# Second layer of a two-layer Mamba block: preparation restructured as a pipeline, accumulating stores spread over the steps, four-state weights two steps ahead

## The chip, the cores and the metric

The kernel runs on one core of a Trainium2 chip (trn2). The metric is the device time of one launch in microseconds (us). The engines are PE (TensorE, with PEld for its weight loads), DVE (VectorE), ACT (ScalarE), POOL (GpSimd) and SP (SyncE, which only issues transfers here). Each works through its own queue in order.

## The reference

Four images of 64 x 64 positions and 192 channels pass through two layers. Each layer normalises groups of channels, projects to 384 inner channels, runs selective scans over four orders of the positions, sums the four results, normalises, gates and projects back. The change lies in the second layer, whose scan is this, run on four orders of the same sequence (rows, rows reversed, columns, columns reversed):

```
x_dbl = u @ W_x
dt, B_mat, C_mat = split(x_dbl)                 # 12, 16 and 16 columns
dt = softplus(dt @ W_dt + b_dt)
A = -exp(A_log)                                 # A[d, n], 16 states n
log_decay = cumsum(dt * A, axis=1)
decay = exp(log_decay)
dB_u = dt * B_mat * u
h = decay * cumsum(dB_u / (decay + 1e-12), axis=1)
y = einsum('bldn,bln->bld', h, C_mat) + u * D   # summed over the four orders
```

The term 1e-12 makes `h` vanish once the decay is small against it. The kernel therefore computes only the first positions of each order: 256 for state 0, 128 for states 1 to 3, 64 for states 4 to 7 and 32 for states 8 to 15. A running maximum, `alive`, records whether that was enough; if not, a slower path at the end recomputes the layer.

## The kernel before

The first layer takes most of the launch, and the change leaves it alone. The second layer, class `SecondLayer`, runs in four stages, each over all four images: `project`, `prepare`, `scans`, `finish`. A tile of [128, 3, 512] holds 384 channels (3 groups of 128 partitions) for 512 positions, which are four stretches of 128, one for each order. An image has two such chunks: M (the first 128 positions of each order) and E (the next 128).

**`project`** ends with convolutions whose result `u` goes out through tiles `du` (L1116, stored by L1119) into `y`, and whose first positions go to the DRAM tensors `uc`.

**`prepare`** turns each of the eight chunks (M and E of four images) into what the scans need. The instructions of one chunk, with their lines, are:

- SP loads `uc` (L1219); PE computes `xp` (L1222, three matmuls over 128 rows), ACT copies it with a bias to `xd` (L1224).
- `delta`, the softplus: PE computes `dp` for each of three channel groups (L1148, over 13 rows); ACT takes `Abs` (L1155), then `Exp` (L1156); POOL makes `wl`, `dt` and a correction (L1159 to L1161); ACT takes `Ln` (L1162); POOL adds (L1163). PE computes the three `dp` a second time, and DVE makes `dt = max(dp, 0) + e` (L1165). The `dp` tiles come from three PSUM buffers, so a `dp` can only be written once the third before it has been read.
- `sums`: DVE's running sum `cum` of `dt` (helper line L977). The E chunk continues from the M chunk's ends. `test` (L1191 to L1194) updates `alive`. DVE forms `e = dt * uc` (L1229).
- `keep`: PE transposes part of `xd` to `bp` (L1201) and the whole of `e` to `tp` (L1209, twelve transposes); ACT copies that to `dtuT` (L1210); SP stores `rows`, `bT`, `dtuT`, `dt` and `cum` in DRAM (L1198 to L1213).

In this stage a scheduler places the instructions on the engines' queues. It starts from the order of the program, which finishes one chunk before it begins the next.

**`scans`** has its order written out by hand. `flat` lists nine steps for each image: states 0, 1, 2, 3 on M one at a time; states 4-5 and 6-7 on S (half stretches); state 0 on E; states 8-11 and 12-15 on Q (quarter stretches). Four states together are called a four-state step here. In step `g` the queues get, in this order:

- `c_rows(g + 2)` (SP loads `bct`, L1320) and `b_product(g + 2)` (ACT, `xT`, L1314);
- `weight(g + 1)` and `decay(g + 1)`, the factors `sg` and `a` of the next step. With one or two states ACT makes them (L1284). With four states POOL first multiplies (L1273, six instructions), and ACT applies the function (L1279);
- for each channel group `d`: `scan(g, d)` on DVE (L1332 and two or four scans of L977), `turn_x(g + 1, d)` on PE (`x`, L1325, in three PSUM buffers), and, two steps behind (`LAG`), PE's sum of the products: `add_y` (`yp`, L1366), or for the E step `ext_y` (`yq`, L1383, copied by ACT to `yte`, L1384);
- `c_product(g)` on POOL (L1348), which multiplies the scan's `h` by `bct`.

Two results go out for each image: `yte` after its E step and `ytm` (copied from `yp` by `end_y`) when all steps are summed, two steps into the next image. Both call `store`, which puts six DMAs with addition on POOL's queue (L1400 for rows, L1403 for columns). They add to overlapping places of the same `y`, so some of them wait until earlier ones have landed.

```python
for k, lo in enumerate((near, near, L - far, L - far)):
    if k % 2 == 0:
        nc.gpsimd.dma_start(ys[b][lo : lo + SEG, :], y[:, k, :], accum_op=ALU.add)
        continue
    for s in range(2):
        nc.gpsimd.dma_start(v[lo // HW + s], y[s * HW : (s + 1) * HW, k, :], accum_op=ALU.add)
```

**`finish`** loads `y` again, normalises it (POOL, L891), gates it and projects it back (L916). Its first load of `y` (L870) was issued right after the last store of the scans had landed.

Of the kernel before, what the change touches and what calls it, by code (L numbers as in the profile page):

```python
# [979 lines left out]
class SecondLayer(FirstLayer):  # L980
# [149 lines left out]
    def prepare(self, ucs, batches):  # L1130
        nc, tc = self.tc.nc, self.tc
        with ExitStack() as ctx:
# [12 lines left out]
            def dt_rows(xd, d):  # L1145
                dp = ps_d.tile([128, LC], F32, name="dp")
                w = self.w_dt[:, 0, d * 128 : (d + 1) * 128]
                nc.tensor.matmul(dp, w, xd[0 : DR + 1, :], start=True, stop=True)  # L1148
                return dp

            def delta(xd):

                e = p3.tile([128, ND, LC], F32, name="e")
                for d in range(ND):
                    nc.scalar.activation(e[:, d, :], dt_rows(xd, d), AF.Abs)  # L1155
                nc.scalar.activation(e, e, AF.Exp, scale=-1.0)  # L1156
                wl = p2.tile([128, ND, LC], F32, name="wl")
                dt = p3.tile([128, ND, LC], F32, name="dt")
                nc.gpsimd.tensor_scalar(wl, e, 1.0, 1.0, ALU.add, ALU.mult)  # L1159
                nc.gpsimd.tensor_scalar(dt, wl, -1.0, 1.0, ALU.add, ALU.mult)  # L1160
                nc.gpsimd.tensor_tensor(e, e, dt, ALU.subtract)  # L1161
                nc.scalar.activation(wl, wl, AF.Ln)  # L1162
                nc.gpsimd.tensor_tensor(e, e, wl, ALU.add)  # L1163
                for d in range(ND):
                    nc.vector.scalar_tensor_tensor(dt[:, d, :], dt_rows(xd, d), 0.0, e[:, d, :], ALU.max, ALU.add)  # L1165
                return dt, e

            def sums(dt, before):

                cum = p3.tile([128, ND, LC], F32, name="cum")  # L1170
                for d in range(ND):
                    for k in range(KD) if before is not None else range(2):
                        w = SEG if before is not None else LC // 2
                        part = slice(k * w, (k + 1) * w)
                        if before is None:
                            scan_add(nc, cum[:, d, part], self.keep[:, part], dt[:, d, part], 0.0, k == 1)
                        else:
                            one = self.one.to_broadcast([128, SEG])
                            scan_add(nc, cum[:, d, part], one, dt[:, d, part], ends(before, d, k), k >= 2)
                return cum  # L1180
# [31 lines left out]
                nc.sync.dma_start(chunk.dram["dt"], dt)  # L1212
                nc.sync.dma_start(chunk.dram["cum"], cum)  # L1213

            for uc_dram, (main, ext, _, _) in zip(ucs, batches):
                before = None
                for r, chunk in enumerate((main, ext)):
                    uc = p2.tile([128, ND, LC], F32, name="uc")
                    nc.sync.dma_start(uc, uc_dram[:, r])  # L1219
                    xp = ps_x.tile([NX, LC], F32, name="xp")  # L1220
                    for d in range(ND):
                        nc.tensor.matmul(xp, self.w_xp[:, d, 0, :], uc[:, d, :], start=(d == 0), stop=(d == ND - 1))  # L1222
                    xd = p2.tile([NX, LC], F32, name="xd")
                    nc.scalar.activation(xd, xp, AF.Identity, bias=self.xbias)  # L1224
                    dt, e = delta(xd)
                    cum = sums(dt, before)
                    before = cum
                    test(cum, r)
                    nc.vector.tensor_mul(e, dt, uc)  # L1229
                    if r == 0:  # L1230
                        for at in (0, SEG, 3 * SEG - 1, 4 * SEG - 1):
                            nc.vector.memset(dt[:, :, at : at + 1], 1e30)
                    keep(chunk, xd, dt, cum, e)


    def scans(self, batches, ys):
        nc, tc = self.tc.nc, self.tc
        with ExitStack() as ctx:
            pool = lambda name, bufs, **k: ctx.enter_context(tc.tile_pool(name=name, bufs=bufs, **k))
            p1, p2, p3, p5 = (pool(f"s{b}", b) for b in (1, 2, 3, 5))  # L1240
            ps_y = pool("psy", 1, space=bass.MemoryType.PSUM)
            ps_x = pool("psx", 3, space=bass.MemoryType.PSUM)
            ps_m = pool("psm", 2, space=bass.MemoryType.PSUM)
# [47 lines left out]

            def weight(g):

                sg[g] = p3.tile([128, ND, LC], F32, name="sg")
                by_state(g, flat[g][0].cum, sg[g], AF.Tanh, 0.5, self.ln_q)

            def decay(g):
                as_[g] = p3.tile([128, ND, LC], F32, name="a")
                by_state(g, flat[g][0].dt, as_[g], AF.Exp)

            def blocks(g):
# [20 lines left out]
            def turn_x(g, d):  # L1322
                xs[g, d] = ps_x.tile([128, LC], F32, name="x")
                for b, (cols, _, _) in enumerate(blocks(g)):
                    nc.tensor.transpose(cols(xs[g, d]), xTs[g][:, b, d * 128 : (d + 1) * 128], ident)  # L1325
# [50 lines left out]
            def ext_y(g, b):  # L1376
                it = flat[g][0]
                if b == 0:
                    it.y = p1.tile([128, NJ, DI], F32, name="yte")
                yq = ps_m.tile([128, LC], F32, name="yq")  # L1380
                for q in range(b * NJ, (b + 1) * NJ):
                    k, d = divmod(q, ND)
                    nc.tensor.transpose(yq[:, q % NJ * 128 : (q % NJ + 1) * 128], hs[g][:, d, k * SEG : (k + 1) * SEG], ident)  # L1383
                nc.scalar.copy(it.y.rearrange("p j e -> p (j e)")[:, b * LC : (b + 1) * LC], yq)  # L1384
                if b == ND - 1:
                    store(it.y, flat[g][2], SEG)

            def end_y(b):
                y = p1.tile([128, NJ, DI], F32, name="ytm")
                for i in range(ND):  # L1390
                    to = y.rearrange("p j e -> p (j e)")[:, i * LC : (i + 1) * LC]
                    (nc.scalar.copy if i == 1 else nc.vector.tensor_copy)(to, yp[i])
                store(y, b, 0)

            def store(y, b, near):
                far = near + SEG
                v = ys[b].rearrange("(h w) e -> w h e", w=HW)
                for k, lo in enumerate((near, near, L - far, L - far)):
                    if k % 2 == 0:
                        nc.gpsimd.dma_start(ys[b][lo : lo + SEG, :], y[:, k, :], accum_op=ALU.add)  # L1400
                        continue
                    for s in range(2):
                        nc.gpsimd.dma_start(v[lo // HW + s], y[s * HW : (s + 1) * HW, k, :], accum_op=ALU.add)  # L1403

            with tc.manual_schedule(engines={nc.tensor.engine, nc.scalar.engine, nc.vector.engine, nc.gpsimd.engine}):
                tc.keep_in_program_order(nc.scalar.preload_act_table_set("exp_and_others"))
                for it in batches[0]:
                    load(it)
                c_rows(0)
                c_rows(1)  # L1410
                b_product(0)
                b_product(1)
                weight(0)
                decay(0)
                for d in range(ND):
                    turn_x(0, d)
                start_y()
                for g in range(N + LAG + 1):
                    b, n = divmod(g, PER)

                    for at, i in ((4, 0), (6, 2), (7, 1), (8, 3)):
                        if n == at and b + 1 < len(batches):
                            load(batches[b + 1][i])
                    if g + 2 < N:
                        c_rows(g + 2)
                        b_product(g + 2)
                    if g + 1 < N:
                        weight(g + 1)
                        decay(g + 1)
                    if n == 3 and 0 < b < len(batches):  # L1430
                        start_y()
                    ready = [g - LAG] if LAG <= g < N + LAG else []
                    if n == LAG and b > 0:
                        ready = []
                    elif n == 3 and b > 0:
                        ready = [g - 3, g - 2]
                    for d in range(ND):
                        if g < N:
                            scan(g, d)
                        if g + 1 < N:  # L1440
                            turn_x(g + 1, d)
                        for q in ready:
                            (ext_y if flat[q][0].name[0] == "E" else add_y)(q, d)
                    if g < N:
                        c_product(g)
                    if n == LAG and b > 0:
                        end_y(b - 1)


@with_exitstack  # L1450
# [126 lines left out]
```

## Time and profile before

| | us |
|---|---|
| median of three runs | 11391.58 (11390.1 to 11404.04) |
| the profiled execution: its own time | 11400.69 |
| its span from first to last instruction | 11398.9 |
| stage `prepare`: first L1148 to last L1210 | 10534 to 10728 |
| stage `scans`: first L1332 to last store | 10746 to 11093 |
| stage `finish` | 11095 to 11399 |

| engine | busy us, share of the span |
|---|---|
| PE | 9629.2 (84%) |
| DVE | 9660.8 (85%) |
| ACT | 9638.7 (85%) |
| POOL | 9049.1 (79%) |

The shares are averages over a launch in which the first layer has the greatest weight. The change touches some 550 us of it, so that stretch is read by itself: which engine waits for which, stage by stage. Times on the trace count from the first instruction. The mean granted clock of PE is 0.926 over the whole span, and lower in the second layer.

### The profile page before, as it was taken

To read this page: it belongs to the slowest core of one execution; us is meant where nothing else is said; L and a number is where in the kernel's file an instruction comes from. 1 tells how busy PE (TensorE), PEld (TensorE's weight loads), DVE (VectorE), ACT (ScalarE), POOL (GpSimd) and SP (SyncE) were. 2 spreads that over 40 slices of the span, in tenths; PEclk is the share of its full clock that TensorE was granted. 3 is DMA by queue.
4 is the path that set the end of the run, shared out by engine and by line. 5 is a ranking of instruction groups with operands and counts; after the bars stand their busy time and mean duration, and the time that the engine had idled before them with its cause. 6 is when DMAs were issued, how large, how long until landed. Compare 5 with 4: busy or idle time off the path is not lost. (4 is left out here: it accounts for less than half of the span.)

```text
span 11398.9 us, 171795 instructions
## 1 busy us (share of the span) xinstructions
PE 9629.2 (84%) x61449; PEld 7328.0 (64%) x61449; DVE 9660.8 (85%) x11508; ACT 9638.7 (85%) x16730; POOL 9049.1 (79%) x3032
## 2 busy tenths in 40 slices
PE   7998888878998888878988888779988888788667
PEld 4776666655776666646766666647766666555356
DVE  4999899966999899948999899849998999788455
ACT  5999999957999999939999999849999999665554
POOL 3999899956999899938999899839998999700468
PEclk8999999988999999988999999979999999889678
DMA  4333334444333334443333334433333443433446
GB/s 125 108 105 97 94 99 98 100 127 122 108 103 100 93 99 99 97 156 97 109 102 96 96 97 103 123 119 108 108 99 94 98 103 98 128 120 127 144 117 238
DMA packets 831027, 1269.85 MB, mean 111 GB/s; under 512 B 99002, under 2 KB 514631, under 8 KB 829652
## 3 DMA queue, kind: packets, MB, share of 16 engines
q1 hardware_dynamic: 825300, 1252.49, 39.3%
q0 software_dynamic: 4864, 6.29, 0.4%
q8 instruction: 488, 8.00, 0.3%
q14 instruction: 375, 3.07, 0.1%
HBM read 958.19 MB, written 300.42 MB: 110 GB/s over the span
## 5 line engine op out<-in xcount | busy, mean ns | idle before, releaser
L738 POOL TENSOR_TENSOR h<-h,bct 128x1536 f32<-128x1536 f32 x2048 | 7062.7, 3470 | 577.6 <-DVE carry L734 475.8
L724 DVE TENSOR_TENSOR_SCAN h<-a,carry,x 128x512 f32<-128x512 f32 x5376 | 6605.9, 1267 | 226.8 <-PE x L716 184.5
L716 PE MATMUL x<-ident,xT 128*128 128x128 f32 x24576 | 4000.0, 287 | 815.7 <-DVE h L724 713.6
L699 ACT ACTIVATE xT<-dtuT,bT 128x384 f32<-128x384 f32 x8192 | 4360.0, 610 | 91.6 <-PE x L716 87.0
L716 PEld LDWEIGHTS x<-ident,xT 128*128 128x128 f32 x24576 | 2803.7, 145 | 2139.0 <-DVE h L724 926.3
L711 ACT ACTIVATE a<-dt,A_log_f 128x512 f32<-128x512 f32 x6144 | 3978.8, 717 | 0.0
L751 PE MATMUL yp<-ident,h 128*128 128x128 f32 x24576 | 3703.4, 277 | 9.3 <-POOL h L738 9.1
L751 PEld LDWEIGHTS yp<-ident,h 128*128 128x128 f32 x24576 | 2945.6, 144 | 78.8 <-issue 63.1
L615 PE MATMUL dp<-xd,w_dtb_f 13*128 13x512 f32 x1536 | 890.1, 663 | 208.0 <-DVE dt L644 206.9
L724 DVE TENSOR_TENSOR_SCAN h<-a,x 128x512 f32<-128x512 f32 x768 | 899.0, 1207 | 191.2 <-PE x L716 113.4
L628 POOL TENSOR_SCALAR wl<-e 128x1536 f32<-128x1536 f32 x128 | 189.3, 1479 | 699.0 <-ACT e L624 381.0
L891 POOL TENSOR_SCALAR yt<-yt,mv,rs 128x384 f32<-128x384 f32 x256 | 466.9, 1837 | 200.1 <-DVE rs L886 187.0
L490 PE MATMUL pp<-xT,w_in 96*128 96x512 f32 x1152 | 536.9, 617 | 0.0
L615 PEld LDWEIGHTS dp<-xd,w_dtb_f 13*128 13x128 f32 x1536 | 238.7, 192 | 452.1 <-DVE dt L644 336.1
L745 PE MATMUL yp<-yold,ident 128*128 128x512 f32 x768 | 440.8, 659 | 72.6 <-DMA yold<-y 72.6
L621 ACT ACTIVATE e<-dp 128x512 f32<-128x512 f32 x384 | 224.8, 585 | 307.8 <-DVE dt L644 153.5
L1094 DVE SCALAR_TENSOR_TENSOR acc<-pad,conv_w_s,acc 128x2048 f32<-128x2048 f32 x192 | 439.2, 2343 | 52.6 <-ACT acc L1092 51.9
L641 POOL TENSOR_TENSOR e<-e,wl 128x1536 f32<-128x1536 f32 x128 | 444.9, 3476 | 0.3
L638 POOL TENSOR_TENSOR e<-e,dt 128x1536 f32<-128x1536 f32 x128 | 442.8, 3459 | 0.3
L905 PE MATMUL vp<-ident,yt 128*128 128x128 f32 x768 | 163.6, 361 | 305.4 <-POOL yt L891 303.6
L1075 POOL MEMSET pad<- 128x66 f32 x12 | 1.9, 159 | 508.1 <-DVE acc L1094 489.3
L490 PEld LDWEIGHTS pp<-xT,w_in 96*128 96x128 f32 x1152 | 222.4, 198 | 253.4 <-issue 244.6
(171 smaller groups left out, 7173.9 us busy)
## 6 DMA issues: line engine op xcount, KB each, us to landing
bct<-xp SPq DMA_DIRECT2D x1024, 512.0 KB, 4.9
uT<-uT SPq DMA_DIRECT2D x64, 768.0 KB, 4.7
yold<-y SPq DMA_DIRECT2D x64, 768.0 KB, 8.0
y<-yt SPq DMA_DIRECT2D x64, 768.0 KB, 4.3
uT<-uT SPq DMA_DIRECT2D x128, 384.0 KB, 5.3
yold<-y SPq DMA_DIRECT2D x128, 384.0 KB, 5.3
y<-yt SPq DMA_DIRECT2D x128, 384.0 KB, 4.6
yt<-y SPq DMA_DIRECT2D x64, 768.0 KB, 10.4
```

The lines of the kernel that those rows point to most:

```text
L490: self.tc.nc.tensor.matmul(pp, self.w_in[:, i, e * 128 : (e + 1) * 128], self.xT[:, i, t * LC : (t + 1) * LC], start=(i == 0), stop=(i == ...
L615: nc.tensor.matmul(self.dp[d], w, self.xd[0 : DR + 1, :], start=True, stop=True)
L638: nc.gpsimd.tensor_tensor(self.e, self.e, self.dt, ALU.subtract)
L641: nc.gpsimd.tensor_tensor(self.e, self.e, self.wl, ALU.add)
L699: nc.scalar.mul(xTs[g][:, j, :], it.dtuT[:, j * DI : (j + 1) * DI], it.bT[:, j, n : n + 1])
L711: nc.scalar.activation(as_[g][:, d, :], it.dt[:, d, :], AF.Exp, scale=scale)
L716: nc.tensor.transpose(xs[g, d][:, j * 128 : (j + 1) * 128], xTs[g][:, j, d * 128 : (d + 1) * 128], ident)
L724: nc.vector.tensor_tensor_scan(along(hs[g][:, d, :], it.k), along(as_[g][:, d, :], it.k), along(xs.pop((g, d)), it.k), 0.0 if it.first els ...
L738: nc.gpsimd.tensor_tensor(hs[g], hs[g], bc(cs[g - n % 2][:, n % 2, :], 1, ND), ALU.mult)
L745: nc.tensor.matmul(it.yp[b], ident, yo, start=True, stop=False, skip_group_check=True)
L751: nc.tensor.matmul(it.yp[b][:, i * 128 : (i + 1) * 128], hs[g][:, d, j * 128 : (j + 1) * 128], ident, start=False, stop=n == NS - 1, is_tr ...
L891: nc.gpsimd.tensor_scalar(part, part, mv[:, i, 0:1], rs[:, i : i + 1], ALU.subtract, ALU.mult)
```

## The change

In `prepare`, what a chunk needs up to POOL's last addition becomes a function `start`, and the loop issues `start` of the next chunk ahead of the rest of the present one. `uc` and `xd` move from the pool of two buffers to that of three. The product `e = dt * uc` now stands before `test`.

In `scans`, `store` returns a list of DMAs instead of issuing them. The lists gather in `stores`, and one DMA is issued after `turn_x` for channel groups 1 and 2 of each step, so two in a step, until the list is empty; what is left after the last step is issued then. A four-state step has its `weight` and `decay` issued two steps ahead, the others one step ahead as before. `sg` and `a` get four buffers instead of three.

```diff
-            def delta(xd):
+            def start(uc_dram, r):
+                uc = p3.tile([128, ND, LC], F32, name="uc")
+                nc.sync.dma_start(uc, uc_dram[:, r])
+                xp = ps_x.tile([NX, LC], F32, name="xp")
+                for d in range(ND):
+                    nc.tensor.matmul(xp, self.w_xp[:, d, 0, :], uc[:, d, :], start=(d == 0), stop=(d == ND - 1))
+                xd = p3.tile([NX, LC], F32, name="xd")
+                nc.scalar.activation(xd, xp, AF.Identity, bias=self.xbias)
                 e = p3.tile([128, ND, LC], F32, name="e")
...
                 nc.gpsimd.tensor_tensor(e, e, wl, ALU.add)
-                for d in range(ND):
-                    nc.vector.scalar_tensor_tensor(dt[:, d, :], dt_rows(xd, d), 0.0, e[:, d, :], ALU.max, ALU.add)
-                return dt, e
+                return uc, xd, e, dt
...
-            for uc_dram, (main, ext, _, _) in zip(ucs, batches):
-                before = None
-                for r, chunk in enumerate((main, ext)):
-                    uc = p2.tile([128, ND, LC], F32, name="uc")
-                    nc.sync.dma_start(uc, uc_dram[:, r])
...
-                    dt, e = delta(xd)
-                    cum = sums(dt, before)
-                    before = cum
-                    test(cum, r)
-                    nc.vector.tensor_mul(e, dt, uc)
...
-                    keep(chunk, xd, dt, cum, e)
+            order = [(b, r) for b in range(len(batches)) for r in range(2)]
+            ready = [start(ucs[b], r) for b, r in order[:1]]
+            for i, (b, r) in enumerate(order):
+                if i + 1 < len(order):
+                    ready.append(start(ucs[order[i + 1][0]], order[i + 1][1]))
+                uc, xd, e, dt = ready.pop(0)
+                for d in range(ND):
+                    nc.vector.scalar_tensor_tensor(dt[:, d, :], dt_rows(xd, d), 0.0, e[:, d, :], ALU.max, ALU.add)
+                before = cum = sums(dt, before if r else None)
+                nc.vector.tensor_mul(e, dt, uc)
+                test(cum, r)
...
+                keep(batches[b][r], xd, dt, cum, e)
...
-                sg[g] = p3.tile([128, ND, LC], F32, name="sg")
+                sg[g] = p4.tile([128, ND, LC], F32, name="sg")
...
-                as_[g] = p3.tile([128, ND, LC], F32, name="a")
+                as_[g] = p4.tile([128, ND, LC], F32, name="a")
...
-                    store(it.y, flat[g][2], SEG)
+                    stores.extend(store(it.y, flat[g][2], SEG))
...
-                store(y, b, 0)
+                stores.extend(store(y, b, 0))
+
+            stores = []
...
+                r = []
                 for k, lo in enumerate((near, near, L - far, L - far)):
                     if k % 2 == 0:
-                        nc.gpsimd.dma_start(ys[b][lo : lo + SEG, :], y[:, k, :], accum_op=ALU.add)
-                        continue
-                    for s in range(2):
-                        nc.gpsimd.dma_start(v[lo // HW + s], y[s * HW : (s + 1) * HW, k, :], accum_op=ALU.add)
+                        r.append((ys[b][lo : lo + SEG, :], y[:, k, :]))
+                    else:
+                        r += [(v[lo // HW + s], y[s * HW : (s + 1) * HW, k, :]) for s in range(2)]
+                return r
+
+            def store_next():
+                to, of = stores.pop(0)
+                nc.gpsimd.dma_start(to, of, accum_op=ALU.add)
...
-                    if g + 1 < N:
-                        weight(g + 1)
-                        decay(g + 1)
+                    for q in (g + 1, g + 2):
+                        if q < N and (q - g == 2) == (len(flat[q][1]) == 4):
+                            weight(q)
+                            decay(q)
...
+                        if d > 0 and stores:
+                            store_next()
...
+                while stores:
+                    store_next()
```

In the instruction queues that result, the second and third `uc` loads stand directly behind the first, all behind the last `du` store; POOL's queue holds two stores, then a product, for six steps after each image's turn; and the second layer's `w_out` is loaded after the last `bct` instead of before the preparation.

More of the change, by code (lines that the diff above doesn't have):

```diff
@@ L1213, in keep @@
                 nc.sync.dma_start(chunk.dram["cum"], cum)
-            for uc_dram, (main, ext, _, _) in zip(ucs, batches):
-                before = None
-                for r, chunk in enumerate((main, ext)):
-                    uc = p2.tile([128, ND, LC], F32, name="uc")
-                    nc.sync.dma_start(uc, uc_dram[:, r])
[L1220 to L1224, printed above, removed]
-                    dt, e = delta(xd)
-                    cum = sums(dt, before)
-                    before = cum
-                    test(cum, r)
-                    nc.vector.tensor_mul(e, dt, uc)
-                    if r == 0:
-                        for at in (0, SEG, 3 * SEG - 1, 4 * SEG - 1):
-                            nc.vector.memset(dt[:, :, at : at + 1], 1e30)
-                    keep(chunk, xd, dt, cum, e)
+            order = [(b, r) for b in range(len(batches)) for r in range(2)]
[9 more added lines that the diff above has]
+                test(cum, r)
+                if r == 0:
+                    for at in (0, SEG, 3 * SEG - 1, 4 * SEG - 1):
+                        nc.vector.memset(dt[:, :, at : at + 1], 1e30)
+                keep(batches[b][r], xd, dt, cum, e)
     def scans(self, batches, ys):
@@ L1239, in scans @@
             pool = lambda name, bufs, **k: ctx.enter_context(tc.tile_pool(name=name, bufs=bufs, **k))
-            p1, p2, p3, p5 = (pool(f"s{b}", b) for b in (1, 2, 3, 5))
+            p1, p2, p3, p4, p5 = (pool(f"s{b}", b) for b in (1, 2, 3, 4, 5))
             ps_y = pool("psy", 1, space=bass.MemoryType.PSUM)
```

## The prediction

> **What bounds the kernel now.** I first cut the span into stretches (the view of busy time by stretch). The diff touches two stages of the second layer only: the preparation, which runs from about 10545 to 10728 us, and the scans, from 10746 to 11060 us. Their columns are: stretch, length, then busy time and instructions of PE, PEld, DVE, ACT and POOL, the granted clock, the DMA share, GB/s.
>
> ```profile
> 10545.00:10728.00 183.00, 123.71 (x246) 51.60 (x244) 71.35 (x190) 76.55 (x93) 78.73 (x32) 0.58 0.35 127
> 10746.00:11060.00 314.00, 216.32 (x1440) 177.92 (x1439) 211.58 (x362) 222.96 (x383) 199.19 (x121) 0.83 0.48 113
> ```
>
> No engine is full in either stretch, so both are bound by waits. In the preparation PE is nearest, at a clock of 0.58.
>
> Second, the timeline of each engine in the preparation, here around one main chunk (start, length, engine, line, operation; the bracket is the idle time before and what ended it):
>
> ```profile
> 10598.21 1.89 DVE L1165 SCALAR_TENSOR_TENSOR dt<-dp,e 128x512 f32<-128x512 f32 x3 [11.56 <-POOL e L1163]
> 10605.70 2.79 PE L1209 MATMUL tp<-ident,e 128*128 128x128 f32 x12 [10.66 <-DVE dt L1232]
> 10608.42 8.04 PE L1148 MATMUL dp<-xd,w_dtb_s 13*128 13x512 f32 x9
> 10617.42 1.47 POOL L1159 TENSOR_SCALAR wl<-e 128x1536 f32<-128x1536 f32 x1 [19.25 <-ACT e L1156]
> 10627.49 1.89 DVE L1165 SCALAR_TENSOR_TENSOR dt<-dp,e 128x512 f32<-128x512 f32 x3 [8.16 <-POOL e L1163]
> ```
>
> The engines take turns: DVE finishes `e`, PE transposes it, only then computes the next chunk's `dp`, ACT makes `e`, POOL works 10 us, DVE begins. That is 29.3 us from DVE to DVE; other chunks take 20. The eight chunks' L1165 go from 10558.23 to 10716.03: 22.5 us a chunk. The `dp` of L1148 cost 0.85 us a pass.
>
> Third, the scans, around the turn to the second image:
>
> ```profile
> 10813.93 1.08 POOL L1400 DMA_DIRECT2D y<-yte  x1 [4.89 <-ACT yte L1384]
> 10818.32 1.69 POOL L1403 DMA_DIRECT2D y<-yte  x2 [3.31 <-DMA y<-yte]
> 10822.60 0.90 POOL L1400 DMA_DIRECT2D y<-yte  x1 [2.59 <-ACT xT L1314]
> 10826.50 1.69 POOL L1403 DMA_DIRECT2D y<-yte  x2 [2.99 <-DMA y<-yte]
> 10827.63 10.79 POOL L1348 TENSOR_TENSOR h<-h,bct 128x1536 f32<-128x1536 f32 x3
> ...
> 10831.70 3.60 PE L1366 MATMUL yp<-ident,h 128*32 128x128 f32 x16 [6.95 <-POOL h L1348]
> ...
> 10836.01 0.70 DVE L1332 SCALAR_TENSOR_TENSOR x<-sg,x 128x512 f32<-128x512 f32 x1 [9.04 <-PE x L1325]
> ...
> 10877.24 0.69 DVE L1332 SCALAR_TENSOR_TENSOR x<-sg,x 128x512 f32<-128x512 f32 x1 [4.66 <-ACT sg L1279]
> ```
>
> Six stores sit together on POOL and wait for each other's landing: 13.7 us. Three products `h` queue behind them, PE waits for a product with the next `x` queued behind it, and DVE idles 9 us. The `ytm` stores do it again (4.2 us), and the late POOL then delivers the four-state `sg` late (4.7 us). One image takes 82.3 us (POOL L1273 first at 10790.23, 10872.04, 10956.55, 11036.65).
>
> **What the Trainium skill says.** "TensorE: Matmul & The Clock Gate", Part 1: after an idle window of some 3.4 us PE runs at half clock, and sustained work restores it. The trace agrees on 0.50 after gaps, but goes further: from 10580 to 10590 PE was busy throughout, mostly with 13-row `dp`, at 0.50. "DMA: Bandwidth & Descriptors", Rules for kernel authors: an accumulating DMA must wait for an earlier one on the same bytes. The trace shows these waits, and the change keeps them. The same page's Anatomy of one DMA — SWDGE (gpsimd) path gives 2.0 us plus bytes at 436 GB/s, an estimate of 2.5 us for a 196 KB row store; here the next store starts 4.1 to 5.2 us after it, and I use that.
>
> **Preparation: the start.** In the new order of instructions the first `uc` load stands behind every `du` store on SP's queue and waits for their landing, with two more `uc` loads and the `rows` stores queued behind it; before, it was issued at 10523.97. The wait for those landings ended at 10543.7 before (first L1155). With two loads fewer in their way I take 10542. Then 4.9 us for the load, `xp` 4.5 (mean of six later ones), `xd` 0.7, three `dp` at half clock 5.1 and one `xp` matmul among them 0.9, `Abs` 0.6, table load 1.3, `Exp` 1.5 and hand-overs 0.5: 10562. ACT then has two `xd` ahead of the first `Ln`, and the second waits for a third `xp` (4.4): `Ln` ends at 10570.5. One POOL add (3.4) later DVE may start, at 10574 against 10558.2: **15.8 lost**.
>
> **Preparation: the rest.** Chunk i+1's `Exp` now needs no transpose of chunk i ahead of it. Work per chunk: POOL 1.47+1.47+3.42+3.42 = 9.8; ACT 0.7+1.8+2x1.28+2x1.48+4x0.48 = 9.9 (the sixteen table loads stay); DVE 8.2 to 8.6; PE 12 passes of `dp` at 0.85 = 10.2, `xp` 4.5, `tp` 2.8, `bp` 0.4 = 17.9. At this clock PE becomes the bound. Two chunks are under way at the start: the second add ends 13.4 after the first (the second chunk's `Exp` stands behind that late `Ln`, then POOL's 10), the third 10 later, the fourth 20 (its `dp` stands behind the transposes of the second). The last four follow PE: 17.9 plus 0.4 of gaps, less 1.5 for `dp` that directly follows `xp` and still finds the full clock (0.68 a pass from 10669.66) = 16.8. Sum 13.4+10+20+4x16.8 = 110.6; then DVE 8.3 and transposes with their copies 3.5: last `dtuT` at 10574+122 = 10696. Before: 10727.6. I round the gain to **30 us**. SP's loads of `uc` are two chunks ahead and land before their `xp`, except the fourth by 2 us, which ACT's order hides. Bounds: with PE at full clock (0.43 a pass: 10 a chunk) the in-order chain `e`, `tp`, `Abs`, `Exp`, POOL, DVE over two chunks gives 13 to 14 a chunk, gain 58; with all `dp` cold and 5 us more at the start, 12. The 13.7 us between the last `dtuT` and the first `xT` are loads, and stay.
>
> **Scans: what POOL must do per image.** Nine products at 3.45 = 31.1; four-state products 4x3.03 = 12.1; twelve stores' issue at 0.87 = 10.4. The new POOL order is two stores, then a product, for six steps; by the semaphores the second of the first two pairs waits for the store just before it, and the third pair's first for a store one product older, so its landing is covered. Waits: `yte` 3.4 and 2.6, `ytm` 4.2 and 3.8: 14. Sum **67.6 us**, POOL without a gap. The others need less: ACT 9x2.0 (`xT`) + 5x3.95 (M, E) + 2x5.4 (S) + 2x2.9 (Q) + 2.1 copies = 57; DVE 8 x 5.9 + 6.9 + 1.7 = 56. So POOL is the next bound.
>
> Step by step from an image's first scan, which ends at 5.0: products end at 11.5, 19.3, 24.4, 33.8, 42.9; then the Q products at 48.9, product at 54.1, Q at 60.1, product 63.6. PE needs a product two steps later, at 18.9 (product 1) to 51.8 (product 5), so the stalls are 2 us or less. But the second Q weight is ready at 61.6 while DVE could start at 51.6 + 1: **two steps ahead is still late**, by some 8 us, because the stores slid between. Scan 8 ends at 67, product 8 at 70.5; next image 67.6 later. Images 2, 3 and 4: gain 82.3-67.6 = 14.7 each, 44. The first image has no stores before it: its Q weights start after product 4 (10782.7) instead of product 5 (10790.2), which takes 6 of the 7.1 us of its DVE stalls. The tail is not shortened: last scan to last landing is product 3.5, six `yte` stores 13.6, landing 3, six `ytm` stores 15, landing 3 = 38, against 36 before (11059.3 to 11095.2): 2 lost. Scans **48**. The fourth `sg` and `a` buffers cost no instruction. The load of `w_out` moves on SP from 10542 to behind the last `bct`, at about 11085 on the old scale; L916 first needs it at 11124, so it costs nothing. The last stage, 304 us, is untouched and starts from that landing.
>
> **Sum.** 30 + 48 = 78; I take 76, as the hand-made schedule leaves out small hand-overs. The profiled execution took 11400.7; it would be 11325. It stands 9.1 above the median 11391.6, so the forecast is 11316.
>
> **Rivals.**
> PE warm: the denser pipeline keeps the full clock, preparation gains 58, sum 104: 11288. For it: clock 1.00 in the last projection slices. Against: 0.50 under continuous `dp`.
> Little from preparation: PE cold, gain 12, and store waits of 5 us each take 12 from the scans: 11391.6-48 = 11344.
> The schedule does not do what it says: new in-order waits in the preparation return its whole gain, and POOL's backlog leaves half of the scans' (24): 11368. Against: the counted PE work fits 18 us a chunk.
> Slower: **store landings inside POOL's product chain.** An image costs 53.6 plus four pair waits w. At the traced mean w = 3.5 it is 67.6; each further microsecond costs 12 over three images. At w = 10 all 76 us are gone, and at 12 the result is 11418. It would need other DMA traffic at the same time (the next image's loads begin in step 4). Against: the longest wait before a store in the trace is 5.0.
>
> **How the numbers follow.** Likeliest case 0.50 at 11316, PE warm 0.16, little from preparation 0.18, schedule 0.08, slower 0.06, the rest within 0.2%. 0.2% is 23 us, about what a measurement of this kernel can tell from no change; the first three cases lie beyond it and the fourth on its edge, half of it each side. Faster 0.88, same 0.06, slower 0.06. Range 11276 to 11360: from just below the warm case, with 10 us for the scans, to beyond the third.
>
> **What would show it.** Right: first L1227 (the old L1165) near 10574, then 17 us a chunk, PE nearly gapless at a clock near 0.6; in the scans 67 to 69 us between an image's first four-state products, POOL stores in pairs with one wait of 3 to 5 us each, DVE waits of 8 us left only before the second Q weight, none of 9 us for `x`. Wrong: a chunk every 13 us with a clock over 0.8; POOL with idle time for DVE in the scans (then ACT at 60 is the bound); store waits over 7 us; or a first L1227 at 10560.

## The result and the profile after

The changed kernel takes **11366.17 us** (median of four runs, 11355.46 to 11368.48), the kernel before took 11397.81 beside it (four runs, 11390.1 to 11410.41). The ratio is 0.9969, with a 95% interval of 0.9952 to 0.9987: 0.3% faster. The forecast was 11316, with a range of 11276 to 11360. The gain is there, but it is 32 us instead of 76, and 11366 lies outside the range.

The two profiled executions (own times 11400.69 before, 11355.46 after, so 45.2 apart) are cut at the same four events: the end of the last `du` copy on ACT, the first `dt` on DVE, the end of the last `dtuT` copy, the first `xT`, and the first load `yt` of the last stage.

| stage | before | predicted change | after |
|---|---|---|---|
| last `du` copy to first `dt` | 19.9 | +15.8 | 31.7 |
| first `dt` to last `dtuT` | 169.4 | -47 | 165.3 |
| preparation, sum of these | 189.3 | -32, taken as -30 | 197.0 |
| last `dtuT` to first `xT` | 13.7 | 0 | 13.6 |
| scans and tail: first `xT` to first `yt` | 353.9 | -48 | 313.0 |

The preparation became 7.7 us longer. The scans became 40.9 us shorter. The rest of the 45.2 lies in code that neither kernel changes (6.9 us up to the last `du` copy, 5.0 in the last stage). Such stretches differ from run to run: over the thirteen traces of this case the first `du` copy begins at 10033 to 10061 us, and the last stage takes 297 to 304 us.

In the profile after, the old L1165 is L1227, the POOL lines L1159 to L1163 are L1166 to L1170, L1209 is L1214, L1273 is L1274, L1279 is L1280, L1332 is L1333, L1348 is L1349, and all stores are L1412.

First the busy time by stretch of the changed kernel: stretch, length, busy time and instructions of PE, PEld, DVE, ACT and POOL, granted clock, DMA share, GB/s.

```profile
10531.00:10729.00 198.00, 124.97 (x272) 53.98 (x272) 122.88 (x192) 80.08 (x98) 83.70 (x32) 0.61 0.35 129
10742.00:11055.00 313.00, 228.71 (x1560) 185.91 (x1560) 212.37 (x364) 227.46 (x392) 212.98 (x132) 0.85 0.54 128
```

Read the first line against that of before: DVE has the same work, and its busy time went from 71 to 123 us. DVE does not do more; its instructions take longer. PE's clock is not the reason: from the first `dt` to the last `dtuT` it was 0.59, and 0.58 before. The timelines of DVE and POOL in the first chunk show which ones.

```profile
10563.05 1.89 DVE L1227 SCALAR_TENSOR_TENSOR dt<-dp,e 128x512 f32<-128x512 f32 x3 [10.93 <-POOL e L1170]
10564.86 8.00 DVE L977 TENSOR_TENSOR_SCAN cum<-keep_s,dt 128x256 f32<-128x256 f32 x6
10572.78 1.73 DVE L1229 TENSOR_TENSOR e<-dt,uc 128x1536 f32<-128x1536 f32 x1
10574.43 4.92 DVE L1196 TENSOR_TENSOR end<-cum,A_max_s 128x6 f32<-128x6 f32 x4
```

```profile
10563.31 1.47 POOL L1166 TENSOR_SCALAR wl<-e 128x1536 f32<-128x1536 f32 x1 [0.28 <-ACT e L1163]
10564.86 1.94 POOL L1167 TENSOR_SCALAR dt<-wl 128x1536 f32<-128x1536 f32 x1
10566.89 3.67 POOL L1168 TENSOR_TENSOR e<-e,dt 128x1536 f32<-128x1536 f32 x1
10572.85 4.97 POOL L1170 TENSOR_TENSOR e<-e,wl 128x1536 f32<-128x1536 f32 x1 [2.29 <-ACT wl L1169]
```

The pipeline does what it was to do: POOL works on the second chunk while DVE works on the first. But the six scans take 8.00 us instead of 3.59, and the four tiny `end` products, 0.36 us before, take 4.92. POOL's last add takes 4.97 instead of 3.4. The three L1227, which read one operand from PSUM, keep their 0.69 us each. The groups by tile give minimum, median and maximum in ns for all chunks, first of before, then of after:

```profile
L977 DVE TENSOR_TENSOR_SCAN cum<-one,cum,dt x48: 455/459/477, 10579.8 to 10722.0; 128x128 f32<-128x128 f32 x48
L977 DVE TENSOR_TENSOR_SCAN cum<-keep_s,dt x24: 666/668/682, 10560.0 to 10691.5; 128x256 f32<-128x256 f32 x24
```

```profile
L977 DVE TENSOR_TENSOR_SCAN cum<-one,cum,dt x48: 447/453/3604, 10586.1 to 10722.8; 128x128 f32<-128x128 f32 x48
L1196 DVE TENSOR_TENSOR end<-cum,A_max_s x32: 146/152/3418, 10574.4 to 10724.9; 128x6 f32<-128x6 f32 x32
L977 DVE TENSOR_TENSOR_SCAN cum<-keep_s,dt x24: 658/1597/3843, 10564.9 to 10710.2; 128x256 f32<-128x256 f32 x24
```

The minimum is as before; the maximum lies some 3.2 us above it, about the length of one POOL `tensor_tensor` (3.43 us). PE pays for it, as its waits in the preparation show (what was waited for; total us, times, longest). The transposes `tp` need `e`; the name `end` stands there because it is the last instruction on DVE before the release.

```profile
PE tp L1214 <- DVE end L1196: 53.0, 6, 12.4
PE xp L1157 <- DMA uc<-uc: 12.0, 2, 10.0
PE tp L1214 <- DVE e L1229: 6.4, 2, 6.2
```

The scans went nearly as foretold. POOL's timeline at the same turn to the second image:

```profile
10809.50 1.07 POOL L1412 DMA_DIRECT2D y<-yte  x1
10814.99 0.84 POOL L1412 DMA_DIRECT2D y<-yte  x1 [4.42 <-ACT a L1285]
10815.57 3.74 POOL L1349 TENSOR_TENSOR h<-h,bct 128x1536 f32<-128x1536 f32 x1
10818.96 1.18 POOL L1412 DMA_DIRECT2D y<-yte  x1
10826.18 0.88 POOL L1412 DMA_DIRECT2D y<-yte  x1 [6.03 <-ACT sg L1285]
10826.76 3.78 POOL L1349 TENSOR_TENSOR h<-h,bct 128x1536 f32<-128x1536 f32 x1
```

Two stores, a product, two stores, a product: each of the first two pairs has one wait inside. Before, no product stood between the six. (The releaser in the bracket is an engine that had long been done; it is the landing of the store before that ends the wait.) The four waits of an image sum to 18.1, 16.6 and 14.2 us over the three turns. The first four-state products of each image begin at 10783.28, 10853.65, 10924.03 and 10993.72, so an image takes 70.1 us on average, instead of 82.1 before.

### The profile page after: what moved, and what is told of

The parts are those of the page before. It is cut to its first block, busy times and chain, and to the rows that moved or that the text cites. A ratio compares the mean times of both kernels' runs of the same rounds, so it can differ in the third digit from the quotient of the medians.

```text
span 11353.7 us, 171741 instructions
## 1 busy us (share of the span) xinstructions
PE 9604.8 (85%) x61449; PEld 7309.5 (64%) x61449; DVE 9710.5 (86%) x11508; ACT 9639.2 (85%) x16730; POOL 9051.8 (80%) x3032
```

## The experiments

All are timed beside the kernel before, with 4 to 21 executions of each. The table has the ratio to it with its interval, and from the profiled execution the three stretches of the table above: start (last `du` copy to first `dt`), rest (first `dt` to last `dtuT`), scans with tail.

| kernel | ratio, interval | start | rest | scans |
|---|---|---|---|---|
| before | 1 | 19.9 | 169.4 | 353.9 |
| after (four runs) | 0.9969, 0.9952 to 0.9987 | 31.7 | 165.3 | 313.0 |
| e_prep_only | 1.0013, 1.0007 to 1.0020 | 29.8 | 168.0 | 354.5 |
| e_scans_only | 0.9958, 0.9944 to 0.9972 | 21.2 | 166.1 | 318.3 |
| e_dt_psum | 0.9934, 0.9921 to 0.9948 | 30.1 | 124.5 | 317.5 |
| e_all_dve | 0.9944, 0.9930 to 0.9957 | 30.2 | 134.3 | 313.9 |
| e_pool_beside | 1.0021, 1.0012 to 1.0030 | 20.0 | 195.5 | 355.8 |
| e_rows_first | 0.9949, 0.9936 to 0.9963 | 29.8 | 166.7 | 286.2 |
| e_two_ahead_only | 0.9995, 0.9987 to 1.0003 | 20.0 | 169.7 | 350.8 |
| e_stores_spread_only | 0.9981, 0.9974 to 0.9988 | 19.9 | 168.7 | 334.9 |
| e_psum_uc_early | 0.9941, 0.9928 to 0.9955 | 30.9 | 126.4 | 312.4 |
| e_psum_rows | 0.9919, 0.9905 to 0.9932 | 35.9 | 129.3 | 286.9 |
| e_best | 0.9913, 0.9898 to 0.9929 | 24.6 | 131.7 | 284.2 |

### The two halves apart

`e_prep_only` has the new `prepare` and the old `scans`; `e_scans_only` the reverse.

> The new preparation with the old scans. Theory A (DVE's instructions with two operands in SBUF stand still while POOL's run, so DVE's 8 us and POOL's 10 us of a chunk still follow each other): no gain, 0 to 10 us slower than before, that is 11390 to 11405 by the median before; stretch from the last du store to the last dtuT 195 to 200 us against 189.3. Theory B (the pipeline works, and what the changed kernel lost it lost elsewhere): 20 to 30 us faster, 11365.

> The old preparation with the new scans. Theory A (the scans hold all the gain): 35 to 45 us faster than before, and 0 to 10 us faster than the whole change. Theory B (both parts give about half): 15 to 20 us faster. First xT to the first yt load 313 us, as with the whole change, either way.

Measured: the new preparation alone is 0.13% slower (11414.02 against 11399.78), with a stretch of 197.8 us. The new scans alone are 0.42% faster (11355.83). Theory A holds for both (the first is 14 us slower, a little more than the 0 to 10 it gave): the preparation's pipeline costs time, and all of the gain is the scans'. So the search narrows to why the preparation did not gain the 30 us that were forecast.

### Who holds whom: one POOL instruction beside DVE's scans

This is the suspected cost by itself, in the kernel before:

```diff
                     nc.vector.scalar_tensor_tensor(dt[:, d, :], dt_rows(xd, d), 0.0, e[:, d, :], ALU.max, ALU.add)
+                nc.gpsimd.tensor_tensor(wl, dt, dt, ALU.add)
                 return dt, e
```

> The kernel before, with one more tensor_tensor of 128x1536 on POOL for every chunk of the preparation: it reads dt as soon as DVE's three L1165 have made it, and writes wl, whose value nobody needs any more. It stands beside DVE's cum scans, and POOL has nothing else to do then. Theory A (a POOL instruction holds up DVE's instructions with two operands in SBUF): one scan of every chunk, or the one behind it, takes 3 us and more instead of 0.46 to 0.68, and the stretch from the last du store to the last dtuT grows by about 3.4 us a chunk, 20 to 30 us over eight, from 189.3. Theory B (DVE and POOL don't disturb each other; what made the scans long under the change was something else): scans stay at 0.46 and 0.67 us, the stretch stays within 3 us.

Measured: 0.21% slower, and the preparation takes 215.4 us instead of 189.3, 26.1 more, or 3.3 for each of the eight chunks. Theory A holds. POOL's extra instruction and DVE's six scans, from the timelines of the two engines in the third chunk:

```profile
10616.83 2.99 POOL L1166 TENSOR_TENSOR wl<-dt 128x1536 f32<-128x1536 f32 x1 [2.06 <-DVE dt L1165]
```

```profile
10614.80 1.89 DVE L1165 SCALAR_TENSOR_TENSOR dt<-dp,e 128x512 f32<-128x512 f32 x3 [9.38 <-POOL e L1163]
10616.60 6.09 DVE L977 TENSOR_TENSOR_SCAN cum<-keep_s,dt 128x256 f32<-128x256 f32 x6
```

Six scans of 3.59 us became 6.09: longer by 2.5 us, while POOL worked for 3.0. Nothing reads POOL's result, and the scans write `cum`, which POOL does not touch. Both read `dt` here, but that is not the reason: in the changed kernel POOL works on the tiles of another chunk. It is POOL's work as such that stands in DVE's way.

### One operand in PSUM

The tail makes `dt` in PSUM, lets the scans (in `sums`) and the product read it there, and copies it to SBUF for its store. The `dp` of the tail get two PSUM banks of their own, so the stage's eight are split 2+2+2+2 instead of 3+2+3.

```diff
...
-                    nc.vector.scalar_tensor_tensor(dt[:, d, :], dt_rows(xd, d), 0.0, e[:, d, :], ALU.max, ALU.add)
-                before = cum = sums(dt, before if r else None)
-                nc.vector.tensor_mul(e, dt, uc)
+                    dp = dt_rows(xd, d, ps_e)
+                    nc.vector.scalar_tensor_tensor(dp, dp, 0.0, e[:, d, :], ALU.max, ALU.add)
+                    sums(cum, d, dp, before if r else None)
+                    nc.vector.tensor_mul(e[:, d, :], dp, uc[:, d, :])
+                    nc.vector.tensor_copy(dt[:, d, :], dp)
...
```

> The whole change, and in the preparation dt is made in PSUM, where the cum scans and the product with uc read it; three copies bring it to SBUF for its store (2 us of DVE a chunk). PSUM banks are split 2+2+2+2. Theory A (two operands in SBUF are what POOL blocks): the cum scans take 0.67 (main) and 0.46 us (E) beside POOL again, as in the kernel before, where their median was 1.60 under the change; DVE and POOL of neighbouring chunks overlap, the stretch from the last du store to the last dtuT falls by 10 to 40 us from 197.0. Theory B (PE at half clock, in order, is the bound of the preparation): the scans still get short, but the stretch stays within 5 us of 197. Theory C (the long scans wait for something else, such as DMA traffic or POOL's data): the scans stay at a median over 1.2 us.

Measured: 11326.26, 0.66% faster than before. The preparation (start and rest) fell from 197.0 to 154.6 us although DVE has three copies more per chunk. The same scans and PE's same waits, from the groups by tile and the waits:

```profile
L977 DVE TENSOR_TENSOR_SCAN cum<-one,cum,dp x48: 446/455/480, 10587.0 to 10693.5; 128x128 f32<-128x128 f32 x48
L1195 DVE TENSOR_TENSOR end<-cum,A_max_s x32: 151/153/2658, 10582.4 to 10695.2; 128x6 f32<-128x6 f32 x32
```

```profile
PE tp L1213 <- DVE e L1230: 15.9, 6, 7.2
```

No scan of 48 takes over 0.48 us now, with POOL busy beside them. The `end` products, which still have both operands in SBUF, still take up to 2.66. PE's wait for DVE ahead of `tp` fell from 59.4 to 15.9 us. Theory A holds (its 10 to 40 us were just exceeded), theory C falls, and theory B falls as well: PE was not what bounded the changed kernel. What bounds this version is not decided. By stretch, from the first `dt` on:

```profile
10573.00:10698.00 125.00, 104.26 (x234) 36.75 (x234) 112.93 (x231) 64.73 (x84) 69.09 (x29) 0.63 0.47 178
```

PE is busy 104 of 125 us, at a clock of 0.63, and DVE 113. POOL still holds part of that: sixteen `max` of 128x1 (`alive`), with both operands in SBUF, take 26 us, and at the usual 0.16 us each would take 2.5. The edit also splits the PSUM banks and orders DVE's work by channel group, so not all of the 42 us need come from the operands; the lengths of the scans do.

### POOL's four operations on DVE

```diff
-                nc.gpsimd.tensor_scalar(wl, e, 1.0, 1.0, ALU.add, ALU.mult)
+                nc.vector.tensor_scalar(wl, e, 1.0, 1.0, ALU.add, ALU.mult)
...
```

> The whole change, with the four elementwise operations of the preparation that POOL ran (about 10 us a chunk there) on DVE. Theory A: nothing on POOL is left to block DVE; the operations take 1 to 1.7 us each on DVE, 4 to 6 a chunk, so the chain of a chunk is 4 to 6 us shorter and DVE needs some 13 us a chunk; the stretch from the last du store to the last dtuT falls by 20 to 60 us from 197.0. Theory B (PE at half clock is the bound, 17 us a chunk): falls by 20 us at most. Theory C (DVE has no time for more): the stretch grows.

Measured: 11339.59, 0.56% faster than before; stretch 164.4 us, 32.6 less than after. On DVE the four take 0.95, 0.95, 1.75 and 1.75 us where POOL takes 1.47, 1.47, 3.43 and 3.43, and every scan has its 0.46 or 0.67 us again. Theory A holds. In this stage giving DVE all the work is better than sharing it with an engine that stops it. This version leaves PSUM as the change has it, so a gain of this kind does not need the split of the banks.

### The two halves of the scans

Both have the old preparation. `e_two_ahead_only` issues the six stores at once as before; `e_stores_spread_only` goes back to weights one step ahead.

> The old preparation and the new scans, with all six stores of a tile issued at once as before; only the four-state weights are two steps ahead. Theory A (POOL's store groups are what the image's time depends on): little, 0 to 10 us faster than before; the stall for the second four-state weight (4.7 us an image) goes but the 9 us waits for x stay. Theory B (the weights two ahead bring most of the 41 us): 20 to 40 us faster.

> The old preparation and the new scans, with the four-state weights one step ahead as before; only the stores are spread, two a step. Theory A (the spread carries the gain): 25 to 40 us faster than before, an image at 71 to 76 us instead of 82. Theory B (without the weights ahead, POOL's backlog returns it): 0 to 10 us faster.

Measured: with the weights alone the interval includes no change (scans 3.1 us shorter); the spread alone brings 0.19%, 21 us (scans 19.0 shorter; an image 76.6, 77.2 and 73.0). Together, on the same old preparation (`e_scans_only`), they bring 35.6 in the scans, and the parts sum to 22. So theory A is right in which part matters, but the spread fell short of its 25 us: in part POOL's backlog gives the gain back, as the second theory B said, and each part needs the other. DVE's waits in the scans say why; first the version with weights two ahead, then the one with stores spread, then the whole change:

```profile
DVE x L1332 <- PE x L1325: 45.5, 11, 11.2
...
DVE x L1332 <- ACT sg L1279: 7.6, 6, 1.3
```

```profile
DVE x L1332 <- ACT sg L1279: 38.8, 8, 11.9
...
DVE x L1332 <- PE x L1325: 5.0, 6, 1.3
```

```profile
DVE x L1333 <- ACT sg L1280: 13.6, 5, 4.0
...
DVE x L1333 <- PE x L1326: 3.5, 3, 1.3
```

Before, the two waits were 43.4 (for `x`) and 20.5 (for `sg`). Early weights take away the second and leave the first. Spread stores take away the first, and the delay returns as the second: POOL, whose stores now lie among its products, reaches the four-state weights late. Only both together cut both.

### Stores without a pair that waits

```diff
-                return r
+                return [r[i] for i in (0, 3, 1, 2, 4, 5)]
```

> The whole change, but the six stores of a tile in the order row, row, column, column, column, column instead of row, column, column, row, column, column. No pair then holds two stores of the same bytes; the columns come a product after the rows. Theory A (in the scans POOL is the bound, with 14 to 17 us of landing waits in its 70.2 us an image): POOL needs 54 to 57 us, ACT at about 60 becomes the bound, so an image takes 60 to 62 us, 25 to 30 us less over three images, and the tail's two serial groups lose one wait each, 6 to 8 us: 30 to 38 us faster than the whole change, about 11330. Theory B (the waits hide beside DVE's and ACT's own work, or the columns now wait as long for the rows): 0 to 10 us faster than the whole change.

Measured: 11341.15, 0.51% faster than before; the scans take 286.2 us, 26.8 less than with the whole change. The same turn on POOL:

```profile
10808.01 1.97 POOL L1412 DMA_DIRECT2D y<-yte  x2
10811.21 3.45 POOL L1349 TENSOR_TENSOR h<-h,bct 128x1536 f32<-128x1536 f32 x1 [1.23 <-DVE end L1346]
10814.87 1.73 POOL L1412 DMA_DIRECT2D y<-yte  x2 [0.20 <-issue]
```

The waits inside the pairs are gone, so theory A holds. It gave too much: an image takes 64.6 us, not 60 to 62, and by the medians this version is 25 us faster than the whole change, not 30 to 38. ACT is busy 58 of 65 us and is not full; DVE still loses single waits of 1 to 2 us to PE and ACT. The tail became 10 us shorter (from the last image's first four-state product to the first `yt`: 51.2 instead of 61.3).

### The early start, and all together

> The version with dt in PSUM, and the uc tiles in a pool of their own that is opened first, so that the first two loads no longer wait for the landing of the last du stores and stand ahead of some of them in SP's queue, as in the kernel before. Theory A (the late start costs what the traces show, first dt 30.1 us behind the last du copy there, 20.0 before): 6 to 12 us faster than with dt in PSUM alone, whose interval against before was 0.9921 to 0.9948. Theory B (PE, which needs 16 us a chunk, takes the lead back or the du stores now land later): 0 to 3 us.

Measured: no gain over `e_dt_psum` (0.9941 against 0.9934, intervals overlapping), and the start is 30.9 us. The size is theory B's, but neither theory had the cause. From ACT's timeline:

```profile
10561.90 1.26 ACT L1160 ACTIVATE xd<-xp,x_bias_s 64x512 f32<-64x512 f32 x2 [5.43 <-DMA uc<-uc]
```

PE made both `xp` by 10557, but the first `xd` then waited until 10561.90 for a transfer of `uc`. The likely reason, argued only, is the last `uc` store of the stage before (issued at 10552.27) and memory that `xd` takes over from there; so `xd` was moved as well, in the last version.

```diff
-            p2, p3 = pool("q2", 2), pool("q3", 3)
+            pu, p2, p3 = pool("qu", 3), pool("q2", 2), pool("q3", 3)
...
-                uc = p3.tile([128, ND, LC], F32, name="uc")
+                uc = pu.tile([128, ND, LC], F32, name="uc")
...
-                xd = p3.tile([NX, LC], F32, name="xd")
+                xd = pu.tile([NX, LC], F32, name="xd")
```

> dt in PSUM and the stores rows first, together. Theory A (the two bounds lie in different stages, so their gains add): preparation 155 us from the last du store to the last dtuT, scans with tail 286 us; 34 us less in the first and 68 us less in the second than before, about 100 us faster, 11300. Theory B (one gain takes from the other, as the earlier scans meet the loads): 70 to 85 us faster.

> As the version with dt in PSUM and the stores rows first, and both uc and xd in a pool opened ahead of the others, so that neither the first loads nor the first xd wait for the memory of the stage before. Theory A (the start was lost to such waits: with uc alone moved, xp ran 10 us earlier but xd then waited for the landing of the last uc store): first dt 20 to 24 us behind the last du copy instead of 30, 6 to 10 us faster than without the pool. Theory B (PE, at 16 us a chunk, sets the end of the preparation whatever the start): 0 to 3 us.

Measured: `e_psum_rows` 11311.41 and `e_best` **11303.10** against 11401.62, so 90 and 99 us faster than before; both beat the kernel before and the changed kernel. The gains of the two stages add up nearly as theory A said for `e_psum_rows`: the scans gain 67.0 us (68 forecast), the preparation 24.1 (34 forecast). `e_best` is 8 us faster still, which would fit its theory A, but between the two the runs do not decide: the intervals overlap. The start is 24.6 us in the last version, but the rest took 131.7 instead of 124.5. The start of `e_psum_rows`, 35.9 us, has the same code as `e_dt_psum` with 30.1: PE's granted clock was 0.58 there against 0.72. Why the clock differs is open.

## Why the prediction was wrong, by its own steps

**The step that failed** is the sum "Preparation: the rest". It set POOL's 9.8 us of a chunk beside DVE's 8.2 to 8.6 and let them overlap at their old lengths, 122 us from the first `dt` to the last `dtuT`. All these lengths came from a stage in which POOL and DVE nearly always took turns. The prediction bounded PE's clock from both sides, and left this one cost unbounded, at nothing. Measured were 165.3 us, as the lengths themselves grew. With the scans and the product out of the conflict the same stretch took 124.5 us (`e_dt_psum`), and 126 to 132 in the three versions built on it, which is within 2 to 10 us of the 122. That PE is the next bound, as the working had it, is not shown by this, since DVE was even busier there.

The trace of before did show the cost, in the few places where POOL began a chunk while DVE was still finishing another. From its timelines of POOL and DVE:

```profile
10656.43 1.47 POOL L1159 TENSOR_SCALAR wl<-e 128x1536 f32<-128x1536 f32 x1 [7.92 <-DVE dt L1232]
10656.55 1.36 DVE L1194 TENSOR_TENSOR alive<-alive,top 128x1 f32<-128x1 f32 x1
10675.50 1.93 POOL L1159 TENSOR_SCALAR wl<-e 128x1536 f32<-128x1536 f32 x1 [7.60 <-ACT e L1156]
10675.99 1.45 DVE L1191 TENSOR_TENSOR end<-cum,A_max_s 128x6 f32<-128x6 f32 x1
```

A `max` of 128x1 took 1.36 us and a product of 128x6 took 1.45, where both usually take 0.16; the second `wl` took 1.93 instead of 1.47. These are small numbers, but they were in the trace that the prediction read.

The mechanism was also to be had elsewhere. The Trainium skill, "SBUF — State Buffer", section "SBUF: two separate sides", says that DVE and GpSimd share one port pair under an exclusive lock: a DVE operation "in a 2-port perf mode, or with two SBUF inputs" and a GpSimd operation that reads SBUF exclude each other for a whole instruction. No step of the prediction used it. Where the runs touch this, they agree. Scans with both operands in SBUF took up to 3.84 us instead of 0.67; with one in PSUM, 0.67 and 0.46; POOL was held in its turn (4.97 instead of 3.4). In the scans' stage `x` is in PSUM, and there the trace of before has no scan of 128x256 over 0.69 us, with POOL busy for 199 of 314 us.

**The start** was to cost 15.8 us and cost 11.7: `uc` did wait for the landing of the `du` stores (PE idle for 10.0 us), but what followed was 4 us shorter than counted.

**The scans** were right in mechanism; two terms were mis-sized. The waits in the pairs were 16.3 us an image instead of 14, so an image took 70.1 instead of 67.6, and three images gained 36.0 instead of 44. The first image gained 7.6 (forecast 6), the tail lost 2.7 (forecast 2). Sum 40.9 instead of 48. The late second weight was right in kind: at the turn to the second image DVE waits of 4.0 us before the first four-state step and 3.0 before the second are left, where 8 before the second were forecast. Two readings of the trace of before were off without much effect: an image took 82.1 us by the four times that are given, not 82.3, and 4.9 of the 13.7 us read as landings of stores were the wait for ACT's copy of `yte`, ahead of the first store, when no earlier one was under way. Finish and the load of `w_out` cost nothing, as said.

**The rivals.** "The schedule does not do what it says" gave 11368, and 11366 was measured; but it is right by two errors that cancel. It named waits of the queues' order for the preparation, and the cause was two engines that stop each other; it gave the scans 24 us, and they brought 41. "PE warm" did not occur (clock 0.61). "Store landings inside POOL's product chain" did not occur: no wait in a pair came near 10 us, the longest was 6.0. Of the signs that the text named, two failed clearly: "PE nearly gapless" (PE waited 59 us for DVE) and "17 us a chunk" (22 from one chunk's first L1227 to the next).

## What to carry to other kernels

Before two engines are set side by side in a sum, look in the trace for places where they do work side by side, however short, and compare the lengths there with the usual ones. Where there are none, the lengths are not known, least of all for DVE with both operands in SBUF beside POOL. Put one operand in PSUM, or give DVE the work, before building a pipeline on the pair. Two delays on one engine can hide each other: cutting one alone moved the wait, and the two edits together were worth more (35.6 us) than their sum (22). Where stores must wait for each other, order them so that the waiting one comes a product later; that one line was worth 27 us in the scans.

## What the runs showed of the hardware

- An instruction of almost no work can be held for as long as the other engine's instruction: a `max` of 128x1 on DVE (0.15 us) took 3.15 beside POOL.
- From the first `dt` to the last `dtuT`, PE's granted clock stayed at 0.59 to 0.63 in the four versions with `dt` in PSUM, though PE was busy for 78 to 86% of that stretch; the prediction had assumed a low clock.
